# A four-layer graph network on one core: step 1's flag products moved to an iteration's end in TensorE's order

## The chip, the cores and the metric

The kernel runs on one core of a Trainium2 chip. The metric is the device time of one execution in microseconds (us); the kernel before has been run three times, and the median counts. A further execution was taken by the hardware profiler; all rows of views come from that one. TensorE does the matrix products, VectorE (DVE) and ScalarE (ACT) the work on rows, GpSimd (POOL) small powers and indirect DMAs, SyncE (SP) only issues DMAs.

## The reference

Four layers work on x (4096 rows of 256) with one adjacency matrix adj (4096 x 4096, zeros and ones), each as x = layernorm(x + layer(x)). Layer 1 is the one that matters here. Cut to it:

```python
for n in range(2):                       # STEPS
    q = Xa @ W1.T @ W2.T;  k = Xa @ W3.T
    probs = softmax(q @ k.T)             # 4096 x 4096
    A = probs where the largest of a row, added up, stay below 0.9, else 0
    A = A / sum(A)
    Xf = R @ Xf                          # R: adj with the unit matrix, rows scaled
    Xa = A @ Xa
    Z = Z + Xf @ U1[n].T + Xa @ U2[n].T
h = layernorm(X + Z)
```

The cut at 0.9 needs, for each row, the largest probabilities in order and their running sum.

## The kernel before

The rows are worked in 32 tiles of 128. Layer 0 comes first, then the two steps of layer 1 (n = 0 and n = 1), then layers 2 and 3. Only step 1 (n = 1) is touched.

**A tile's way in step 1.** `run_step` (L941) loops over i from -2 to 31, and three tiles are under way in each iteration. For tile i + 2 TensorE forms the logits (`logits_chunk`, L411), which ScalarE copies into a row block e (L412). For tile i + 1 VectorE looks for the largest values: `peak_groups` takes eight from each of 16 stretches (L430), `exp_rows` lets ScalarE form the exponentials (L453), `tops` takes the 64 largest in eight rounds (L525, L529), and `pick` adds them up and finds the threshold, how many equal values are too many, and whether the row can't be settled from 64 values. That last answer is `bad` (L561), one number for each of the 128 rows. `flag` and `settle` follow, see below. For tile i, whose e is settled by then, TensorE turns e by transposes (`turn`, L741; ScalarE copies the result, L744) and multiplies it with all rows of Xa (L766). `after` then mixes the result with U1 and U2 (L819, VectorE L821), two layer norms follow (L191 to L202, with GpSimd's power at L197), and the rows are written out. In the same iteration the product with adj (`neighbours`, L683, ScalarE's cast L680) for one tile is worked in.

**The order within an iteration.** `pieces` (L720) goes through eight groups, g = 0 to 7. In each it writes the logits of the group, the next group's transposes, the product of this group, and the group of adj; after that it calls what was entered for g by `at(g, ...)` in `run_step`. In step 1 the mix of the tile before is entered at 1, the next query (L391) at 1, `exp_rows` at 1, `tops` and `pick` at 2, `flag` at 4, `settle` at 5. A put-off job advances at 1 and 6.

**Flag and settle.** Rows with `bad` set are put off: they are gathered later, 128 at a time. `flag` (L579) must give each such row a place in a list. Two products of TensorE count them over the 128 rows: L589 with a matrix of ones (how many in the tile) and L590 with a triangle `before` (how many before this row). Both go into a half of one bank, `mm_bank`, whose halves are used in turn by queries, mixes and flags. VectorE forms the new total `sofar` (L592), `slot` (L596) and `slots` (L597), and GpSimd writes the row numbers into the list in memory by an indirect DMA (L603). `settle` (L638) does not need the counts: it removes surplus equal values from e (L655), and keeps what is over the threshold in four passes (L660). In step 1 the list is read at four points: after i = 7, 15, 23 and 30 `put_off` (L894) takes `base` from the total (L898), SyncE reads 128 entries (`take_rows`, L885), VectorE bounds them (L887), GpSimd gathers the rows (L809). Such a job then has its own query, logits, peak (L468), five probes (L495), tops, flag (L585) and settle, spread over the following iterations; its product comes at the next of the four points, for the last two after the loop. Beside those last two, TensorE has 32 products for layer 2 (`zu_tile`, L868).

**What sets the order on an engine.** The program is written in one order; the framework then plans a fixed order for each engine ahead of the run. It goes by an estimate of times: among the instructions that it takes to be ready, the one written earliest is placed next. So an instruction may stand earlier on its engine than it is written. `tc.keep_in_program_order(ins)` adds an edge without a semaphore: `ins` is placed behind the instruction of its engine that was written just before it.

Of the kernel before, what the change touches and what calls it, by code (L numbers as in the profile page):

```python
# [54 lines left out]
def gnn_stack(ctx, tc, x, adjt, adjn, w0, b0, w1, w2t, w3t, u1t, u2t, ln_g, ln_b, w2, b2, w3, b3, out):  # L55
# [3 lines left out]
    nc = tc.nc  # L59
# [3 lines left out]
    NLC = N // LC  # L63
# [20 lines left out]
    def half(bank):  # L84
        turns[bank] ^= 1
        return (mm_bank if bank == "mm" else acc_bank)[:, turns[bank], :]
# [90 lines left out]
    def transposed(*srcs):  # L177

        n = 2 * len(srcs)
        ps = ps_tr.tile([P, 4, P], F32, tag="tr", name="tr")  # L180
        for s, src in enumerate(srcs):
            for c in range(2):
                nc.tensor.transpose(ps[:, 2 * s + c, :], src[:, c * P : (c + 1) * P], ident)  # L183
        t = work.tile([P, 4, P], F32, tag="xt", name="xt")
        nc.scalar.copy(t[:, :n, :], ps[:, :n, :])  # L185
        return t
# [165 lines left out]
    with tc.tile_pool(name="l1", bufs=1, reuse_waits="tile") as l1:  # L352

        cur = {"late": False, "n": 0, "nef_done": False}
# [4 lines left out]
        ones_sq = l1.tile([P, P], F32, name="ones_sq")  # L359
# [25 lines left out]
        def query(xi, xt=None):  # L385

            if xt is None:
                xt = transposed(xi)
            ps = half("mm")
            for c in range(2):  # L390
                nc.tensor.matmul(ps[:, :P], wq_sb[:, c, :], xt[:, c, :], start=(c == 0), stop=(c == 1))  # L391
            up = upper(ps[:, :P])
            q = [work.tile([P, P], F32R, tag=f"q{k}", name=f"q{k}", bufs=3) for k in range(2)]
            nc.scalar.copy(q[0], up)
            nc.vector.tensor_sub(q[1], ps[:, :P], up)
            return q
# [17 lines left out]
        def logits_in(l):  # L414

            nc.vector.memset(l[:, N:], -1.0)
            return l

        def small(tag, w=1, dt=F32, bufs=2):
            if cur["late"]:  # L420
                return cur["lw"].tile([P, w], dt, tag=tag, name=f"{tag}_l", bufs=2 if w == 1 else 1)
            return work.tile([P, w], dt, tag=tag, name=tag, bufs=bufs)
# [34 lines left out]
        def peak_groups(st):  # L457

            st["cand"] = cand = small("cand", 8 * ngr, bufs=1)
            groups(st["e"], cand)  # L460
            st["m"] = m = small("m")
            nc.vector.tensor_reduce(m, cand, axis=AX.X, op=ALU.max)
            nc.vector.tensor_scalar(m, m, -1.0, None, op0=ALU.mult)
            st["base"] = None
# [114 lines left out]
        def flag(st):  # L579


            pb = half("mm")
            later = st.get("later")
            if later is None:
                nc.tensor.matmul(pb[:1, 0:1], st["bad"], ones_col, start=True, stop=True)  # L585
                st["nb"] = small("nbad", 1, I32)[:1, :]
                nc.scalar.copy(st["nb"], pb[:1, :1])
                return
            nc.tensor.matmul(pb[:, 0:1], ones_sq, st["bad"], start=True, stop=True)  # L589
            nc.tensor.matmul(pb[:, 1:2], before, st["bad"], start=True, stop=True)  # L590
            sofar, slot = small("sofar"), small("slot")
            nc.vector.tensor_add(sofar, later["base"], pb[:, 0:1])  # L592

            i = st["tile"]
            at, rows_i = slots_of[cur["n"]][:, i : i + 1], ids[:, i : i + 1]
            nc.vector.scalar_tensor_tensor(slot, pb[:, 1:2], later["base"], spare, op0=ALU.add, op1=ALU.subtract)  # L596
            nc.vector.scalar_tensor_tensor(at, slot, st["bad"], spare, op0=ALU.mult, op1=ALU.add)  # L597
            later["base"] = sofar
            if i == NT - 1 and cur["n"] == 0:

                st["to"] = to = small("to_last", 1, I32, 1)
                nc.vector.scalar_tensor_tensor(to, st["bad"], float(P), rows_i, op0=ALU.mult, op1=ALU.add)
            nc.gpsimd.indirect_dma_start(  # L603
                out=list_d[cur["n"]], out_offset=bass.IndirectOffsetOnAxis(ap=at, axis=0), in_=rows_i, in_offset=None)
# [316 lines left out]
        def left_over(n, e, later):  # L921

            count = work.tile([P, 1], I32, tag="count_l", name="count_l", bufs=1)
            nc.vector.tensor_scalar(count, later["base"], float(P - 1 - LATER[n] * P), 0.0, op0=ALU.add, op1=ALU.max)
            nc.vector.tensor_scalar(count, count, P.bit_length() - 1, None, op0=ALU.arith_shift_right)
            v = nc.values_load(count[0:1, 0:1], min_val=0, max_val=NT - LATER[n])
            with tc.For_i(0, v, 1) as k:
                cur["late"] = True
                st, xg = take_rows(n, bass.ds(k * P + LATER[n] * P, P), e)
                all_logits(st, query(xg))  # L930
                peak(st)
                exp_rows(st)
                st["t"], st["left"], st["base"] = small("t_thr"), small("left"), None
                for _ in settle(st, True):
                    pass
                pieces(n, st, None, {})
                for f in after(n, st):
                    f()
                cur["late"] = False

        def run_step(n, es):  # L941
# [37 lines left out]
            for i in range(-2, NT):  # L979
                st = tiles.pop(i, None)  # L980
                cd = tiles.get(i + 1)
                nxt = None
                if i + 2 < NT:

                    nxt = {"tile": i + 2, "q": cur["qs"].pop(0), "e": logits_in(es[i % 2]), "later": later, "G": {}}
                    tiles[i + 2] = nxt
                if i + 1 == NT and n == 0:
                    for fs in last:
                        for f in fs:
                            f()  # L990
                    last = []
                    left_over(n, es[NT % 2], later)
                ops = {}

                def at(g, f, *args):
                    ops.setdefault(g, []).append(lambda: f(*args))

                for g, fs in zip((1, 2), last):
                    for f in fs:
                        at(g, f)  # L1000
                if 0 < i + 2 < NT - 1:
                    turned = []
                    g = 1 if n else 6
                    at(g - 1, lambda i, turned: turned.append(transposed(cur["xa"][:, i + 3, :])), i, turned)
                    at(g, lambda turned: cur["qs"].append(query(None, turned[0])), turned)
                if cd is not None:
                    peak_groups(cd)
                    at(1, exp_rows, cd)
                for job in jobs:
                    at(1, advance, job)  # L1010
                if cd is not None:
                    rounds = 8 if n else KEPT // 8
                    at(2, tops, cd, rounds)
                    at(2, pick, cd, rounds)
                    at(4, flag, cd)
                    if n == 0:
                        for k in range(8):
                            at(4 + k // 2, gather, cd, k)
                    else:
                        at(5, lambda cd: [None for _ in settle(cd)], cd)  # L1020
                for job in jobs:
                    if n and i + 1 == NT:
                        at(4, advance, job)
                    at(6, advance, job)
                if i + 1 == NT and n == 0:
                    cur["next"] = load_halves(es[1 - NT % 2], xf_d, nc.sync)
                if i < 0:
                    now = FIRST[n][i + 2]
                else:
                    now = [i + 2] if FIRST[n][1][-1] < i + 2 < NT else []  # L1030
                pieces(n, st, nxt, ops, now)
                last = [[f] for f in after(n, st)] if st is not None else []
                if i in starts:
                    k = starts[i]
                    if len(jobs) > (i == NT - 2):
                        last = finish(jobs.pop(0), last)
                    e = es[NT % 2] if k + 1 == LATER[n] else es[2]
                    jobs.append({"stages": put_off(n, k, e, later)})
                    if i < NT - 2:
                        advance(jobs[-1])  # L1040
# [185 lines left out]
```

## Time and profile before

| what | value |
|---|---|
| median of three runs | 3284.64 us (3282.99 to 3286.56) |
| profiled execution | 3212.81 us |
| its span, first to last instruction | 3211.1 us |
| mean granted TensorE clock in it | 0.97 |
| step 1's flag products, first and last start | 1389.6 and 2503.2 us |
| instructions L589 and L590 in both steps | 128 each (two passes a tile, 64 tiles) |

A view's row names the line of the kernel, the engine and the operation, then the tiles as out<-in; "x" is a count. PE is TensorE's matmuls and PEld its weight loads, which overlap them. In a timeline row the first number is the start in us from the span's start and the second the time taken; neighbouring instructions of a kind are one row. In brackets stands how long the engine was idle before it and what ended that. In the rows by stretch, each engine's busy time is followed by its count of instructions; after the five engines come the granted clock, the share of the DMA engines and GB/s. A line of a helper (L149, L183 and others) serves many callers.

### The profile page before, as it was taken

Reading aid. Unit: us, or ns where it says so; the run is one execution under the profiler, and the core shown is the slowest. Engines: PE = TensorE matmul, PEld = TensorE weight load, DVE = VectorE, ACT = ScalarE, POOL = GpSimd, SP = SyncE. Lnnn points to the kernel's source line nnn. Section 1 sums busy time; section 2 is a strip of 40 time slices with the busy share of each in tenths; the row PEclk is TensorE's granted clock in tenths of the full one; section 3 lists DMA queues with packets and bytes.
Section 4 is the critical chain, followed back from the end, with each engine's and each line's share of the span. In section 5 each row is a group of like instructions: output and inputs, shape, how many; then the busy total and the mean of one; then the engine's idle time right before and its main releaser. Section 6 shows DMA issues by size and latency. Waiting matters only on the chain. (4 is left out here: it accounts for less than half of the span.)

```text
span 3211.1 us, 45754 instructions
## 1 busy us (share of the span) xinstructions
PE 2949.0 (92%) x14376; PEld 2329.4 (73%) x14376; DVE 2289.4 (71%) x7161; ACT 1745.9 (54%) x2906; POOL 786.8 (25%) x915
## 2 busy tenths in 40 slices
PE   8999889999999996799989899989999796999998
PEld 3788667777777774578877777877788554887886
DVE  4666778888888875269979896988799664444444
ACT  3555655666666654365545454545555334666664
POOL 1121256677666763000000001000100100000000
PEclk9999999999999998899999999999999898999999
DMA  9995467777778774310001110111011234333332
GB/s 175 164 173 117 83 114 141 144 143 143 141 142 150 152 140 118 118 50 25 24 24 27 34 39 24 32 32 37 29 35 27 71 119 139 109 108 101 106 110 81
DMA packets 247872, 300.14 MB, mean 93 GB/s; under 512 B 34688, under 2 KB 201536, under 8 KB 247616
## 3 DMA queue, kind: packets, MB, share of 16 engines
q0 software_dynamic: 46576, 104.94, 22.9%
q1 hardware_dynamic: 188800, 180.93, 18.4%
q10 hardware_dynamic: 12240, 11.23, 1.1%
q8 instruction: 116, 1.90, 0.2%
q14 instruction: 140, 1.15, 0.2%
HBM read 331.17 MB, written 66.45 MB: 124 GB/s over the span
## 5 line engine op out<-in xcount | busy, mean ns | idle before, releaser
L683 PE MATMUL acc_r<-xh,adjq 128*128 128x512 f32 x2048 | 608.5, 428 | 27.7 <-ACT adjq L680 18.6
L766 PE MATMUL acc_bank<-xa,at 128*128 128x256 f32 x2304 | 565.6, 386 | 27.9 <-ACT at L744 27.3
L669 POOL DMA_INDIRECT G<-x_d,cols x512 | 496.1, 969 | 262.6 <-PE acc_bank L758 154.1
L680 ACT CAST adjq<-adj 128x512 fp32r<-128x512 fp8e4 x512 | 316.5, 620 | 386.5 <-PE acc_r L683 308.2
L766 PEld LDWEIGHTS acc_bank<-xa,at 128*128 128x128 f32 x2304 | 422.3, 193 | 88.2 <-ACT at L744 38.7
L683 PEld LDWEIGHTS acc_r<-xh,adjq 128*128 128x128 f32 x2048 | 376.0, 191 | 123.1 <-ACT adjq L680 45.4
L197 POOL TENSOR_TENSOR rstd<-ve,mhalf 128x1 f32<-128x1 f32 x168 | 103.1, 614 | 1337.8 <-DVE ve L195 1270.5
L430 DVE MAX8 cand<-e 128x8 f32<-128x256 f32 x1024 | 382.9, 415 | 65.0 <-ACT e L412 63.7
L412 ACT COPY e<-lg 128x512 f32<-128x512 f32 x552 | 319.5, 585 | 195.8 <-PE lg L411 191.9
L411 PE MATMUL lg<-kS,q 128*128 128x512 f32 x1104 | 398.2, 446 | 4.6 <-ACT e L412 4.5
L1106 ACT CAST a<-a 128x1024 fp32r<-128x1024 fp8e4 x256 | 267.9, 1048 | 156.7 <-PE acc L173 121.3
L758 PE MATMUL acc_bank<-G,dg 128*128 128x256 f32 x1024 | 288.5, 399 | 61.8 <-DMA G<-x_d,cols 48.2
L527 DVE FIND_INDEX8 cols<-top,e 128x8 uint32<-128x4096 f32 x64 | 282.8, 4419 | 0.0
L758 PEld LDWEIGHTS acc_bank<-G,dg 128*128 128x128 f32 x1024 | 195.1, 196 | 117.8 <-DMA G<-x_d,cols 65.9
L173 PE MATMUL acc<-xh,a 128*128 128x512 f32 x1024 | 255.0, 402 | 20.2 <-DMA a<-adj_d 15.5
L173 PE MATMUL acc<-y0h,a 128*128 128x512 f32 x1024 | 253.6, 401 | 0.0
L173 PEld LDWEIGHTS acc<-xh,a 128*128 128x128 f32 x1024 | 190.6, 189 | 63.8 <-ACT xh L149 23.0
L173 PE MATMUL acc<-yh,a 128*128 128x512 f32 x1024 | 233.7, 390 | 0.0
L744 ACT COPY at<-at_ps 128x512 f32<-128x512 f32 x296 | 173.5, 588 | 98.7 <-PE at_ps L741 97.0
L173 PEld LDWEIGHTS acc<-yh,a 128*128 128x128 f32 x1024 | 192.2, 188 | 39.6
L173 PEld LDWEIGHTS acc<-y0h,a 128*128 128x128 f32 x1024 | 188.1, 188 | 42.0 <-issue 0.6
L185 ACT COPY xt<-tr 128x256 f32<-128x256 f32 (+1 forms) x268 | 111.9, 425 | 189.8 <-PE tr L183 172.8
(287 smaller groups left out, 4588.0 us busy)
## 6 DMA issues: line engine op xcount, KB each, us to landing
adj<-adj_d SPq DMA_DIRECT2D x256, 128.0 KB
a<-adj_d SPq DMA_DIRECT2D x256, 128.0 KB
a<-in_adjt POOLq DMA_DIRECT2D x64, 256.0 KB
adj_d<-a SPq DMA_DIRECT2D x64, 256.0 KB
adjn<-in_adjn POOLq DMA_DIRECT2D x64, 256.0 KB
x_d<-x SPq DMA_DIRECT2D x64, 128.0 KB
xf_d<-xf_new SPq DMA_DIRECT2D x64, 128.0 KB
G<-x_d,cols POOLq DMA_INDIRECT x512
```

The lines of the kernel that those rows point to most:

```text
L173: nc.tensor.matmul(acc, a[:, j, :], halves(jt), start=(jt == 0), stop=(jt == NT - 1))
L411: nc.tensor.matmul(pl[:, :LC], q[k], kS[:, s], start=(k == 0), stop=(k == 1))
L412: nc.scalar.copy(l[:, s], pl[:, :LC])
L430: nc.vector.max(dst[:, 8 * g : 8 * g + 8], src[:, g * GW : (g + 1) * GW])
L527: nc.vector.max_index(st["at"][:, 8 * r : 8 * r + 8], t8, st["e"][:, :N])
L669: nc.gpsimd.indirect_dma_start(out=g, out_offset=None, in_=x1_d, in_offset=bass.IndirectOffsetOnAxis(ap=st["at"][:, k : k + 1], axis=0))
L680: nc.scalar.copy(a, cur["a8"][:, g % 2 * GP : (g % 2 + 1) * GP, :])
L683: nc.tensor.matmul(acc_r, a[:, j, :], xf[:, jt, :], start=(jt == 0), stop=False)
L744: nc.scalar.copy(at[:, :G, :], ps[:, :G, :])
L758: nc.tensor.matmul(acc_a, dg[:, k % 4, :], st["G"][k], start=(k == 0), stop=(k == KEPT - 1))
L766: nc.tensor.matmul(acc_a, ats[g][:, j, :], cur["xa"][:, jt, :], start=(jt == 0), stop=(jt == NT - 1))
L1106: nc.scalar.copy(a, a8)
```

## The change

In step 1 `flag` is entered at group 7, the last of an iteration, instead of group 4; step 0 keeps 4. And in step 1 the first of its two products is kept behind the TensorE instruction written just before it. The second product is not kept so. No instruction is added or removed. With `flag` go its VectorE operations and its list entry, which are now written behind `settle`.

```diff
@@ flag
-            nc.tensor.matmul(pb[:, 0:1], ones_sq, st["bad"], start=True, stop=True)
+            total = nc.tensor.matmul(pb[:, 0:1], ones_sq, st["bad"], start=True, stop=True)
+            if cur["n"]:
+                tc.keep_in_program_order(total)
             nc.tensor.matmul(pb[:, 1:2], before, st["bad"], start=True, stop=True)
@@ run_step
-                    at(4, flag, cd)
+                    at(NLC - 1 if n else 4, flag, cd)
```

## The prediction

> **What bounds the kernel now.** I read the page first. TensorE is the busiest engine of the whole span, and the slices say that this holds almost everywhere:
>
> ```profile
> PE 2949.0 (92%) x14376; PEld 2329.4 (73%) x14376; DVE 2289.4 (71%) x7161; ACT 1745.9 (54%) x2906; POOL 786.8 (25%) x915
> ```
>
> The change can only touch step 1, which by its first and last flag product runs from 1389.6 to 2503.2 us. So I next asked who TensorE waited for between 1340 and 2530 us (columns: waiting line, releaser, us in total, times, longest):
>
> ```profile
> PE acc_bank L766 <- ACT at L744: 26.7, 15, 5.7
> PE mm_bank L589 <- DVE bad L561: 26.1, 17, 11.1
> ...
> PE at_ps L741 <- DVE e L660: 6.5, 1, 6.5
> ```
>
> The product that is to be moved (L589) is the second largest wait there: 26.1 us in 17 waits. One of them is 11.1 us; the other 16 sum to 15.0 us, some 0.95 us each. Then I listed each of the 32 products with its neighbours. The first ten tiles never wait (their `bad` is 11 us old or more). The waits stand in the iterations that also carry a put-off job. This is one of them on the timeline (start, us, engine, line; in brackets the idle time before it):
>
> ```profile
> 2359.22 0.14 DVE L561 SCALAR_TENSOR_TENSOR bad<-left,bad 128x1 f32<-128x1 f32 x1
> ...
> 2359.42 0.38 PE L589 MATMUL mm_bank<-bad,ones_sq 128*128 128x1 f32 x2 [1.00 <-DVE bad L561]
> ...
> 2359.89 1.54 PE L766 MATMUL acc_bank<-xa,at 128*128 128x256 f32 x6
> 2360.06 0.16 DVE L592 TENSOR_TENSOR sofar<-sofar,mm_bank 128x1 f32<-128x1 f32 x1 [0.23 <-PE mm_bank L590]
> ...
> 2361.32 4.43 DVE L655 MATCH_REPLACE8 e<-match,e 128x4120 f32<-128x4120 f32 x1
> ...
> 2366.01 1.27 DVE L660 SCALAR_TENSOR_TENSOR e<-e,t_thr 128x1024 f32<-128x1024 f32 x1
> ...
> 2369.12 0.60 PE L741 MATMUL at_ps<-ident,e 128*128 128x128 f32 x4
> ```
>
> TensorE stands 1.00 us for `bad`, and only 9.2 us after it the next iteration starts with the transposes of the same tile's e (2369.12), whose first quarter VectorE finished at 2367.28: 1.8 us in hand. In eleven such tiles (10, 14, 15, 18 to 23, 28, 29) that margin is 0.2 to 0.7 us. So **a second wait on VectorE stands close behind the first**. The busy times from one flag product to the next say how full the engines are (columns: stretch, us, then PE, PEld, DVE, ACT busy):
>
> ```profile
> 1488.47:1516.94 28.47, 26.99 (x143) 22.67 (x142) 25.57 (x89) 15.01 (x25) 2.23 (x3) 1.00 0.09 24
> 1780.22:1820.84 40.62, 34.61 (x169) 28.52 (x169) 33.15 (x108) 19.29 (x32) 2.23 (x3) 0.96 0.24 33
> ...
> 2359.42:2395.50 36.08, 34.94 (x177) 29.20 (x177) 35.26 (x118) 19.07 (x33) 2.23 (x3) 1.00 0.11 34
> 2395.50:2431.15 35.65, 34.56 (x178) 28.98 (x178) 34.47 (x115) 19.64 (x34) 2.24 (x3) 1.00 0.12 38
> ```
>
> The first row is an early tile: TensorE is the bound. The last two are tiles with a job: VectorE is busy 35.26 of 36.08 us, more than TensorE. The second is a third kind: both have gaps (6.0 and 7.5 us), each waiting for the other in turn. VectorE's own waits in step 1 name this, and a further one:
>
> ```profile
> DVE h L821 <- PE mm_bank L819: 33.6, 12, 6.6
> ...
> DVE from_l L887 <- DMA to_l<-list_d: 15.1, 3, 5.4
> ```
>
> **What the skill says.** The Trainium skill, "PSUM — Partial Sum Buffer", section "Engine vs sequencer instructions": matmuls start and complete in program order. The trace agrees: the L766 behind the flag products starts at 2359.89, at once behind them, though its operands were there. "Perfetto Trace Analysis", section "Identifying the Most-Contended Engine": the engine to relieve is the one with the highest occupancy, and it can change over time; the rows above show such a change. "DMA: Bandwidth & Descriptors", section "Anatomy of one DMA — SWDGE (gpsimd) path": some 2.0 us of fixed cost for such a DMA. Here the trace differs for the list entry: issued by GpSimd at 1935.66, SyncE's read of the list behind it went out at 1943.62, some 8 us, and that is the figure I use.
>
> **The change part by part.** (1) **Flag products moved and pinned.** Nothing is added or removed: four matmuls per tile (L589 and L590, 2 passes each) cost 0.47 us of TensorE (2359.42 to 2359.89) before and after. They go from behind group 4 to behind group 7 of 8, in the trace about 8 us later (1488.47 against the next tile's first transpose at 1496.37). By then `bad` is 8 us old, so their wait is gone: **15.0 us of TensorE idle time is the most that can be had**. The 11.1 us wait is not part of it: the last 16 matmuls of that iteration (L766 from 2487.86) already stand before that product, so it is at the iteration's end now; behind it the transposes wait another 6.5 us for e. Only settling is late there.
>
> (2) **VectorE's order.** sofar, slot, slots (0.16, 0.21, 0.20 us) are now written behind settle instead of before it. Their wait for TensorE (0.23 us) goes too, as TensorE has finished the products by the time settle's four passes end (tile 19: transposes at 2062.13, last pass at 2065.20). So e comes 0.6 us earlier (0.57 us of small operations plus 0.23 of wait, less what they overlap). TensorE comes to the transposes 1.0 us earlier, e 0.6: with 0.2 to 0.7 us in hand the new wait at L741 is 0 to 0.2 us at first.
>
> (3) **What is late next.** In the seven VectorE-bound iterations (from 1702.80, 2017.89, 2054.32, 2324.81, 2359.42, 2395.50, 2431.15) its work per tile stays, and only its 0.25 us wait can go: 7 x 0.25 = 1.8 us. TensorE runs ahead until the margin at L741 is used, and waits there. In the nine others with a flag wait both engines have gaps, and a TensorE that is earlier brings L819 earlier, for which VectorE waits (33.6 us in 12). Per tile that is worth nothing at the least and 1.0 us at the most; I take the 0.6 us by which e is earlier: 9 x 0.6 = 5.4 us. Sum: **7.2 us**.
>
> (4) **List and queues.** GpSimd's list entry (L603) is moved by the 8 us, with settle in front of it: past one or two small powers (L197, 0.6 us each), which it could delay by its 1.0 us; the value is 0.3 us a tile at VectorE, hidden where TensorE bounds, and I take 0 (bounds 0 and 3 us). At the put-off starts (i = 7, 15, 23, 30) the list's read on SyncE (L885), VectorE's L887 and GpSimd's gather hang on that entry. The first gather, at 1642.12, would go out at 1650; the job's query stands at 1661.47, so 11 us of cover against 8. At the last start the gather moves from 2514.55 to some 2524, its query (2526.03) by 1 to 3 us; behind it the job's e was ready at 2617.3, and TensorE came for it at 2628.08: 10 us cover. Without that cover it would be 3 us. (5) **Half banks.** The next query writes the half that sofar and slot read. It stands 13 us behind the boundary (2074.95 against 2062.13): hidden; up to 1 us a tile without.
>
> (6) **Planning.** The framework plans every engine's order anew from the first moved product. No row prices this; like iterations (34.3 to 36.4 us with equal work) differ by 1 us, over 20 of them some 4 us either way. I take 0.
>
> The profiled execution took 3212.81 us (span 3211.1 and 1.7 around it); less 7.2 it gives 3205.6. The median of the runs is 3284.64, 2.2% longer, which no view explains; with 7.2 x 1.022 = 7.3 us the forecast is **3277.3 us**.
>
> **Rivals.** *VectorE is the pace throughout*: the wait only moves to L741, worth 1.8 to 4 us: 3281 to 3283. For it: the margins of 0.2 to 0.7 us. Against: VectorE's 33.6 us of waiting for TensorE. *Slower, by the late list entry*: L885 and L887 are planned on an estimate of the list's DMA that is already 5 us short (waits of 5.4, 5.3, 4.4 us; TensorE then idles 5.7, 6.2 and 2.7 us behind ScalarE, which waits for VectorE). If the entry goes 8 us later and L887 keeps its place, each start costs up to 8 us more, half of which TensorE's queued work covers: 3 x 4 and 3 at the last start, 15 us, less 5 of gain: 3295 us. It decides once L887's waits reach some 10 us each. Against it: L887 is planned behind the entry, and should move with it. *It doesn't do it*: only L589 is pinned; L590 needs the same `bad`, and may be planned early in its stead. Then 3284.6. Against: L590 now follows L589 in all 32 tiles.
>
> **How the numbers follow.** Forecast 0.58 (own range 3270 to 3282), VectorE's pace 0.14, late list 0.24, no effect 0.04. A measurement can tell about 0.2%, 6.6 us. Of the forecast's 0.58, 0.42 lie beyond it and 0.16 within; so faster 0.42, same 0.16 + 0.14 + 0.04 = 0.34, slower 0.24. Low end: all 15.0 us and 3 of planning, 3267. High end: the late list with 2 of planning, 3297.
>
> **What would show it.** Right: L589's wait falls to the one near 2500 us, L592's vanish, L741's wait for L660 grows from 6.5 to between 8 and 15 us, and L821's 33.6 us shrinks. Wrong: L887's waits over 10 us, L590 waiting for `bad`, or iterations of 1400 to 1630 us (28.2 us each, not touched in my sum) that change length.

## The result and the profile after

| | before | after |
|---|---|---|
| median | 3285.6 us (8 runs, 3281.6 to 3297.8) | 3273.33 us (8 runs, 3262.3 to 3279.2) |
| ratio | | 0.9954, 95% interval 0.9936 to 0.9972 |
| profiled execution | 3212.81 us | 3274.57 us |

The kernel is faster: by 12 us in the medians, by 0.46% in the ratio of the runs, whose interval leaves out 1. Forecast were 7.3 us. The two profiled executions say the opposite at first sight, 3212.81 against 3274.57 us. That comes from ahead of the change: step 1's first transposes start at 1348.8 us in the one and at 1415.3 in the other, although step 0 is planned alike in both (TensorE has the same order there). So only step 1 is compared below, from those transposes to the first product of layer 2: 1334.7 us in this profile of before, 1340.1 in a second one, 1329.4 after.

In the kernel after, lines from L590 on stand two further down (L592 is the second flag product, L594 `sofar`, L662 settle's passes, L743 the transposes, L889 the list's bounds). TensorE's waits from 1406 to 2596 us, the same part of the kernel as before (waiting line, releaser, us, times, longest):

```profile
PE acc_bank L768 <- ACT at L746: 26.7, 14, 6.2
PE mm_bank L589 <- DVE bad L561: 16.6, 6, 11.1
...
PE at_ps L743 <- DVE e L662: 13.6, 9, 6.5
PE tr L183 <- DMA xf_new<-xa_d,from_l: 6.4, 1, 6.4
```

The flag product waits 5.5 us in five tiles, beside the 11.1 at the end, where it waited 15.0 in 16. The transposes' wait for e has grown from 6.5 us in one to 13.6 in nine. And a row is new: TensorE waits 6.4 us, once, for rows that GpSimd gathers for a put-off job. VectorE's waits of the same time:

```profile
DVE h L823 <- PE mm_bank L821: 37.1, 9, 9.5
DVE from_l L889 <- DMA to_l<-list_d: 19.5, 4, 7.3
...
DVE sofar L594 <- PE mm_bank L592: 2.3, 8, 0.8
```

The list's wait grew from 15.1 to 19.5 us, the longest from 5.4 to 7.3; that for the flag products is down to 2.3. The tile whose end the prediction showed at 2359.42, in the timeline of after:

```profile
2426.68 1.28 DVE L662 SCALAR_TENSOR_TENSOR e<-e,t_thr 128x1024 f32<-128x1024 f32 x1
...
2428.52 0.39 PE L687 MATMUL acc_r<-xh,ident_r 128*128 128x512 f32 x1
...
2428.75 0.28 PE L589 MATMUL mm_bank<-bad,ones_sq 128*128 128x1 f32 x2
...
2428.89 0.36 PE L592 MATMUL mm_bank<-bad,before 128*128 128x1 f32 x2
...
2429.11 0.64 PE L743 MATMUL at_ps<-ident,e 128*128 128x128 f32 x4
...
2431.49 0.17 DVE L594 TENSOR_TENSOR sofar<-sofar,mm_bank 128x1 f32<-128x1 f32 x1
...
2432.71 1.02 POOL L605 DMA_INDIRECT list_d<-ids,slots  x1 [14.15 <-DVE slots L599]
```

The products stand last in the iteration, right ahead of the next transposes. Neither they nor `sofar` wait. The list entry now goes out behind settle's four passes.

### The profile page after: what moved, and what is told of

Same layout as the page of the kernel before. It is cut to its first block, busy times and chain, and to the rows that moved or that the text cites. A ratio compares the mean times of both kernels' runs of the same rounds, so it can differ in the third digit from the quotient of the medians.

```text
span 3272.8 us, 45751 instructions
## 1 busy us (share of the span) xinstructions
PE 2970.0 (91%) x14376; PEld 2333.9 (71%) x14376; DVE 2290.0 (70%) x7161; ACT 1744.8 (53%) x2906; POOL 782.6 (24%) x915
## 5 line engine op out<-in xcount | busy, mean ns | idle before, releaser
L685 PE MATMUL acc_r<-xh,adjq 128*128 128x512 f32 x2048 | 620.0, 432 | 32.1 <-ACT adjq L682 18.8
L430 DVE MAX8 cand<-e 128x8 f32<-128x256 f32 x1024 | 383.9, 417 | 85.1 <-ACT e L412 49.5
L173 PE MATMUL acc<-xh,a 128*128 128x512 f32 x1024 | 256.1, 403 | 20.5 <-DMA a<-adj_d 16.4
L411 PEld LDWEIGHTS lg<-kS,q 128*128 128x128 f32 x1104 | 184.5, 193 | 34.0 <-ACT e L412 11.2
```

The source lines that it names most:

```text
L173: nc.tensor.matmul(acc, a[:, j, :], halves(jt), start=(jt == 0), stop=(jt == NT - 1))
L411: nc.tensor.matmul(pl[:, :LC], q[k], kS[:, s], start=(k == 0), stop=(k == 1))
L430: nc.vector.max(dst[:, 8 * g : 8 * g + 8], src[:, g * GW : (g + 1) * GW])
L685: nc.tensor.matmul(acc_r, a[:, j, :], xf[:, jt, :], start=(jt == 0), stop=False)
```

## The experiments

All kernels below keep the line numbers of before, as the pin is written on L589's own line. Ratios are to the kernel before on the same chip, with 95% intervals; its medians were 3247.7, 3283.4, 3284.5 and 3248.3 us on the four occasions. "Step 1" is the stretch named above, from the run's profile. The "starts" are the put-off starts, i = 7, 15, 23 and 30, after which the list is read. In e4 to e10 the first product is pinned in all of step 1, also where flag stays at group 4. There the pin changes next to nothing: in e5, TensorE's order from tile 8 to 24 is the one of before, instruction for instruction.

| run | edit against before | ratio | step 1, us |
|---|---|---|---|
| e1 | none | 1.0004 (0.9991 to 1.0018) | 1340.1 |
| e2 | the change | 0.9960 (0.9946 to 0.9974) | 1326.9 |
| e3 | flag right behind settle, no pin | 1.0025 (1.0012 to 1.0039) | 1350.2 |
| e4 | change, starts stay at 4 | 0.9944 (0.9923 to 0.9965) | 1318.3 |
| e5 | change for i from 24 only, no start | 0.9986 (0.9974 to 0.9999) | 1334.9 |
| e6 | change for 8 to 23 only, no start | 0.9931 (0.9910 to 0.9953) | 1316.8 |
| e7 | change, starts at 3 | 0.9922 (0.9900 to 0.9943) | 1316.4 |
| e8 | flag at 3 everywhere, pinned | 0.9954 (0.9935 to 0.9974) | 1325.7 |
| e9 | flag at 4, starts at 3, pinned | 0.9976 (0.9962 to 0.9991) | 1328.9 |
| e10 | change for 17 to 22 only | 0.9969 (0.9956 to 0.9982) | 1328.4 |
| e11 | before, adj fetched in halves | 0.9936 (0.9913 to 0.9959) | 1329.8 |
| e12 | change, adj fetched in halves | 0.9914 (0.9891 to 0.9936) | 1317.8 |

**e1 and e2: before and after once more, on one chip.** No edit, and the change with the pin written as one line:

```diff
-            nc.tensor.matmul(pb[:, 0:1], ones_sq, st["bad"], start=True, stop=True)
+            total = nc.tensor.matmul(pb[:, 0:1], ones_sq, st["bad"], start=True, stop=True); cur["n"] and tc.keep_in_program_order(total)
...
-                    at(4, flag, cd)
+                    at(NLC - 1 if n else 4, flag, cd)
```

> The kernel before, unchanged, for a second profile of it. It asks whether the profile of before, 3211 us long where its timed runs took 3283 to 3298, is typical in step 1. The stretch from the first transpose of the keys (L1087) to the first product of layer 2 was 1334.7 us in before and 1329.4 us in after, 5.3 us less, where the medians differ by 12.3 us. Theory A (the gain lies in step 1 alone, 5 to 8 us, and the rest of the 12.3 is scatter of step 0, whose order on every engine is the same in both kernels): the second profile shows 1333 to 1337 us again for this stretch, and a step 0 that is some 66 us longer than in the first profile. Theory B (the first profile was short in step 1 too): 1340 us or more. Time against before: 1.000.

> The changed kernel again, written so that the line numbers stay those of before. Theory A: the stretch from the keys to layer 2 takes 1328 to 1331 us, 4 to 7 us less than in the kernel before beside it, and the median is 5 to 8 us lower (ratio 0.9975 to 0.9985). Theory B: the ratio is 0.9955 again and the stretch 10 to 15 us shorter than in the kernel before beside it.

Theory B held in both: 1340.1 us, and 13.2 us less with the change. The gain is real and nearly twice the forecast. I then cut step 1 where `bad` of a tile is ready. Tiles 0 to 8 take 243.2 (e1) and 244.3 us (e2): nearly unchanged. The largest piece is tiles 18 to 24. Here is their row of before (e1, the first block) and of the change (e2, the second) (stretch, us, then busy PE, PEld, DVE, ACT, POOL with counts; granted clock, DMA share, GB/s), and above it the one from tile 16 to 17, below it tiles 26 to 31:

```profile
1961.49:1990.11 28.62, 21.75 (x105) 18.32 (x106) 20.62 (x76) 10.15 (x15) 4.02 (x4) 0.88 0.05 14
2050.49:2270.54 220.05, 206.04 (x1014) 168.44 (x1014) 200.46 (x677) 116.45 (x196) 15.03 (x18) 0.98 0.15 35
2358.00:2535.78 177.78, 161.22 (x823) 134.69 (x823) 173.05 (x575) 87.58 (x148) 12.89 (x15) 0.98 0.12 30
```

```profile
1963.22:1993.11 29.89, 23.78 (x124) 20.32 (x124) 22.54 (x85) 11.22 (x17) 6.04 (x7) 0.94 0.12 22
2050.39:2262.69 212.30, 203.23 (x1026) 168.58 (x1025) 201.46 (x678) 116.23 (x197) 13.41 (x18) 0.99 0.17 35
2352.54:2529.78 177.24, 159.57 (x821) 134.55 (x820) 172.65 (x574) 87.61 (x148) 12.09 (x15) 0.98 0.14 30
```

Tiles 26 to 31 are VectorE-bound (173 of 178 us) and give 0.5 us, as little as forecast. Tile 16 to 17, behind a put-off start, costs 1.3 us more. Tiles 18 to 24 give 7.7. This is no scatter of one execution: before in its two profiles has 219.4 and 220.0 us there, after and e2 212.4 and 212.3. (The stretch from tile 10 to 16 does scatter: 229.3 us in after and 225.6 in e2, which are one and the same change. So no weight is put on it. Tiles 8 to 10 and tile 17 to 18 are some 3 us shorter each with the change and tiles 24 to 26 are 2.3 us longer, in both profiles of either kernel; no run takes these apart.)

The 7.7 us are not to be taken to the tenth. In e5, e8 and e9 TensorE has the order of before in tiles 18 to 24 too, and takes 216.8, 220.2 and 217.4 us there. The row of e5:

```profile
2082.70:2299.51 216.81, 203.65 (x1014) 166.77 (x1014) 200.44 (x677) 116.37 (x196) 15.00 (x18) 0.99 0.15 36
```

So the old order scatters by 3.4 us between executions, and the new one is 4.4 to 7.9 us shorter. What TensorE waited for in tiles 18 to 24, in e1 and in e2:

```profile
PE acc_bank L766 <- ACT at L744: 7.8, 3, 3.8
PE mm_bank L589 <- DVE bad L561: 5.1, 5, 1.2
```

```profile
PE acc_bank L766 <- ACT at L744: 3.3, 1, 3.3
PE at_ps L741 <- DVE e L660: 2.9, 4, 1.0
PE mm_bank L589 <- DVE bad L561: 1.6, 2, 1.1
PE mm_bank L585 <- DVE bad_l L561: 1.3, 1, 1.3
```

This is the surprise. The flag wait gives 3.5 us, and 2.9 of it is paid again at L741 and 1.3 at a job's own flag: **nothing is left of it**. What is gained between these two profiles is 4.5 us of another wait, L766 for ScalarE's copy at L744, and 2.8 us of busy time with nearly the same work (206.0 to 203.2). The wait holds in all: it is 6.4 to 7.8 us in the five profiles with the old order and 3.3 and 3.4 with the change. The busy time doesn't: it is 203.7 us in e5 with the old order. The timeline of before shows where such a wait comes from:

```profile
2163.80 6.76 PE L683 MATMUL acc_r<-xh,adjq 128*128 128x512 f32 x27
2170.39 1.04 PE L741 MATMUL at_ps<-ident,e 128*128 128x128 f32 x8
2171.18 0.48 PE L683 MATMUL acc_r<-xh,adjq 128*128 128x512 f32 x1
2175.46 0.80 PE L766 MATMUL acc_bank<-xa,at 128*128 128x256 f32 x1 [3.79 <-ACT at L744]
```

```profile
2168.92 0.62 ACT L680 CAST adjq<-adj 128x512 fp32r<-128x512 fp8e4 x1 [0.43 <-PE acc_r L683]
2174.30 0.62 ACT L680 CAST adjq<-adj 128x512 fp32r<-128x512 fp8e4 x1 [4.76 <-DMA adj<-adj_d]
2174.83 0.58 ACT L744 COPY at<-at_ps 128x512 f32<-128x512 f32 x1
```

The first block is TensorE, the second ScalarE. At the iteration's boundary the plan of before puts 27 adj products in a row (35 from the last product with Xa to the transposes). They use up the tiles of adj that had been fetched, ScalarE's next cast waits 4.76 us for the next one, and the copy that TensorE needs stands behind that cast. With the flag moved, the plan comes out differently: its four longest such runs in these tiles, ahead of a transpose or a product with Xa, are 14, 18, 27 and 43 products, where they were 22, 24, 35 and 59. The 2.8 us of busy time are the clock: it stands at half speed for 10.2 us in these tiles before (3.4 and 6.8, beginning at 2133.0 and 2173.9, each within or right behind one of the two longer L744 waits) and for 3.4 us with the change. In e5 and e9, with the old order, it is 3.4 and 6.8 us, so the clock's part is not shown to come from the change. The Trainium skill has this in "TensorE: Matmul & The Clock Gate", section "What's actually happening": the clock goes to half after an idle window of some 3.4 us and back after a busy one. The traces agree with the length: pieces of half speed in step 1 are multiples of 3.41 us, from 3.41 to 20.48. But here a wait of 2.8 us, less than the window stated, was followed by half speed too (2133.0).

**e3: the late place without the pin.** The flag is written behind settle in group 5, and its products may be placed early.

```diff
-                    at(4, flag, cd)
+                    n or at(4, flag, cd)
...
-                        at(5, lambda cd: [None for _ in settle(cd)], cd)
+                        at(5, lambda cd: [None for _ in settle(cd)], cd); at(5, flag, cd)
```

> Step 1's flag at group 5, written right behind settle, not pinned: VectorE's order of the change (settle first, then sofar, slot, slots), with TensorE's products only one group later than before. Theory of the wait (the gain comes from TensorE no longer standing for bad): TensorE's place is nearly that of before, so L589 still waits 10 us or more in short waits, and at most a third of the gain is there: 0 to 3 us. Theory of VectorE's order (the gain comes from e being ready 0.6 us earlier in the tiles that are bound by it): half of the gain or more, 4 us and up, with L592 no longer waiting. Theory of the plan (any new order of step 1 moves the time by some us): anything from 8 us faster to 8 us slower, without relation to either wait.

It is 8 us slower: outside what the theories of the wait and of VectorE's order gave, and at the edge of planning's range. L589 still waits 23.1 us in step 1 and L592 10.5; L887 waits 19.6 for the list, as with the change. L821's wait rose from 34.9 to 43.3 us. The late place without the pin gains nothing; how much of the loss is the list isn't taken apart.

**e4 and e7: the put-off starts keep their early list entry.**

```diff
-                    at(4, flag, cd)
+                    at(NLC - 1 if n and i not in starts else 4, flag, cd)            # e4
+                    at((3 if i in starts else NLC - 1) if n else 4, flag, cd)        # e7
```

> The change, but in the four iterations after which the list is read (i = 7, 15, 23, 30) flag stays at group 4, as before. In the profile of after, VectorE's waits for the list (L887 there) grew from 15.1 to 19.4 us, and TensorE got a new wait of 6.4 us for the gathered rows at the first of these points. Theory of the late list entry (my rival, as a part of the truth: it takes back some of the gain): the wait for gathered rows is gone, L887's waits fall to 15 us or less, and the kernel is 4 to 8 us faster than the change. Against it: VectorE's wait is planned behind the entry and moves with it, so that nothing is to be had: within 2 us of the change.

> As the run with the list's points at group 4, but flag stands at group 3 in those four iterations. Theory of the late list entry: the list's read at i = 7 and 23 still waited 5.9 and 5.1 us there, and an entry one group (3 to 4 us) earlier takes that much off each wait and 2 to 5 us off the time (ratio 0.9930 to 0.9940). Rival (VectorE's wait is planned behind the entry and moves with it; what the four iterations gave came from TensorE's place): L887's waits stay at 5 to 6 us, same time within 2 us.

e4: an early list entry at the starts gains. Step 1 is 8.6 us shorter than in e2, L887's wait falls from 19.4 to 11.0 us, and tile 16 to 17 takes 23.7 us for 29.9. The ratios (0.9944 and 0.9960) say the same with less weight, as their intervals overlap. But the gain is more than the change had lost there: in e1 tile 16 to 17 takes 28.6 us. At that start the entry goes out 6.0 us behind its `bad` in e1, 11.6 in e2 and only 1.6 in e4, so e4 doesn't just put back the place of before. TensorE's wait for the gathered rows is gone as well, but with little effect: a wait of 6.2 us for L744's copy stands there instead (6.4 in e1), and tiles 8 to 10 take 80.1 us for 81.4. Tiles 24 to 26, behind the third start, stay at 90.4 us for 89.9, so what they lost is not the list. e7 added nothing that can be told: L887's waits are 5.7, 4.5 and 0.5 us, 10.7 for 11.0. What is left there doesn't hang on the entry. Its ratio is the lowest of the moves of flag, but from another chip than e4's, and the intervals overlap.

**e5, e6 and e10: the change for some tiles alone.** The condition in front of `else 4` is, in this order:

```diff
+                    at(NLC - 1 if n and i >= 24 and i not in starts else 4, flag, cd)
+                    at(NLC - 1 if n and 8 <= i < 24 and i not in starts else 4, flag, cd)
+                    at(NLC - 1 if n and 17 <= i <= 22 else 4, flag, cd)
```

> Flag at group 7 only in the last tiles (i from 24 on, but not at i = 30); before that at group 4 as in the kernel before. In these tiles VectorE is busy 97% of the time; with the change their flag waits went from 4.4 us to none, and the stretch from tile 26 to tile 31 still took 177.2 us against 177.8. Forecast's theory (where VectorE is the bound, taking TensorE's wait away gives only VectorE's own wait of 0.25 us a tile): 0 to 2 us faster than before, ratio 0.9994 to 1.0000. Rival (each flag wait that goes is a microsecond won, wherever it stands): 4 us or more, ratio 0.9988 or less.

> Flag at group 7 only for i from 8 to 23, not at i = 15 and 23; elsewhere at group 4. These tiles hold 11 of the 16 short flag waits and those iterations in which TensorE and VectorE wait for each other. Forecast's theory (the gain comes from the tiles in which both engines have gaps): all of what flag at group 7 with the list's points at group 4 gave (ratio 0.9944), within 2 us: 0.9940 to 0.9955. Rival (the gain is spread over all tiles, or comes from the early tiles' order): half of it or less, ratio 0.9972 or more.

> Group 7 (pinned) only for i = 17 to 22, six iterations in which TensorE and VectorE wait for each other in turn; all others stay at 4. If the wait that is removed is what gains, those tiles give back the 7 to 8 us that they gave in the change's own profile (tiles 18 to 24: 220.0 us to 212.3), with the half-speed time there falling from 10 us to 3 or 0: ratio 0.9970 to 0.9980. By the prediction's own term (0.6 us each) it is 3.6 us, ratio 0.9985 to 0.9992. The four starts stay as they are before: L887's waits 15 to 17 us.

e6 has all of the gain: 0.9931, below the range given, though its interval reaches into it. e10 has the forecast gain with six iterations alone: 0.9969, tiles 18 to 24 take 212.1 us, and the half-speed time there is 3.4 us. Its L887 waits 16.4 us, as before. That shows where the gain lies, but not that it is the flag wait's: in these tiles of e10 the flag wait is 3.5 us less than in e1, 3.0 us are paid at L741, and the 7.8 us of waiting for L744 are gone, with 2.7 for late casts (L683) in their place. e5 is unclear by its time: 0.9986, with an interval that reaches nearly to 1. In its profile the VectorE-bound tiles 26 to 31 take 178.2 us, no less than the 177.8 of before, so they are not where a gain could come from.

**e8 and e9: earlier instead of later.**

```diff
-                    at(4, flag, cd)
+                    at(3 if n else 4, flag, cd)                          # e8
+                    at((3 if i in starts else 4) if n else 4, flag, cd)  # e9
```

> The opposite of the change: in step 1 flag at group 3, one group earlier than before, pinned. Theory of TensorE's wait: TensorE comes to L589 one group (3.5 us) earlier in all 16 tiles with a wait, so the short waits grow from 15 us to 40 us or more, and what VectorE can't give back is lost in the tiles with gaps on both sides: 4 to 15 us slower, ratio 1.001 to 1.005. Rival (VectorE sets the time of bad, TensorE's work behind it fits in later, so that the wait's size is of no matter): within 3 us of before, though the waits grow.

> Only the iterations of the put-off starts (i = 7, 15, 23, 30) get flag a group earlier (3 for 4); all others stay at 4. If the earlier list entry at the starts is what made group 3 everywhere faster by 0.46%, this does the same: ratio 0.9945 to 0.9970, L887's waits fall from 16.5 us to about 11, and the stretch from tile 16 to 17 from 28.6 us to below 25. If that gain came from the other tiles, or from planning as a whole, the ratio is 0.9980 to 1.0010 here, though L887's waits fall alike.

e8 refuted both of its theories: 0.46% faster with L589's waits still at 27.9 us, not over 40. In the tiles that wait, the plan places the product where `bad` is ready, at 3 as at 4; so the flag wait stayed, and the gain has another source. e9 looked for it in the starts. Its row from tile 16 to 17:

```profile
1994.33:2015.74 21.41, 20.89 (x111) 17.87 (x112) 20.49 (x75) 10.59 (x15) 3.24 (x4) 1.00 0.07 19
```

28.62 us in e1 are 21.41 here, as in e8 (21.40): TensorE's idle time fell from 6.9 to 0.5 us and the clock from 0.88 to 1.00 of full. L887 waits 10.9 us. The ratio of 0.9976 lies between the two forecasts, and its interval meets both; the profile's mark is met. An earlier entry at the starts goes with 7 us in one place: it goes out 1.6 us behind `bad` here at i = 15, for 6.0 in e1. It is not shown to be all of e8's gain: tiles 8 to 10 take 81.9 us in e8 and 84.2 in e9, for 84.5 in e1.

**e11 and e12: take away the late adj.** In step 1 a tile of adj holds one group instead of two, in six buffers for three, so the same memory is given back in smaller parts.

```diff
-            if g % 2 == 0:
-                cur["a8"] = cur["w"].tile([P, 2 * GP, P], F8, tag="adj8", name="adj8", bufs=3)
-                nc.sync.dma_start(cur["a8"], adj8_d[i][:, g * GP : (g + 2) * GP, :])
+            if g % (w := 2 - cur["n"]) == 0:
+                cur["a8"] = cur["w"].tile([P, w * GP, P], F8, tag="adj8", name="adj8", bufs=6 // w)
+                nc.sync.dma_start(cur["a8"], adj8_d[i][:, g * GP : (g + w) * GP, :])
...
-            nc.scalar.copy(a, cur["a8"][:, g % 2 * GP : (g % 2 + 1) * GP, :])
+            nc.scalar.copy(a, cur["a8"][:, g % w * GP : (g % w + 1) * GP, :])
```

> The kernel before, flag at 4 and no pin, but in step 1 the tiles of adj are fetched one group at a time into six half-size buffers instead of two groups into three, so that the same memory is given back and filled again earlier; VectorE's and GpSimd's orders stay as they are, TensorE's nearly. Theory C (much of the change's gain in tiles 18 to 24 is not the flag wait, which only moves to e, but two ScalarE casts that wait for adj while TensorE waits behind them, and the half-speed stretch after each): L680's waits for adj fall from 24.3 us to below 12, TensorE's for L744 from 29.0 to below 22, tiles 18 to 24 from 220 us to 211 to 215, with L589's waits still at 26, ratio 0.990 to 0.997. If the flag wait itself is what gained, tiles 18 to 24 stay at 218 to 220 us and the ratio is 0.999 to 1.002.

> The change together with the finer fetch of adj. Theory C: the change and the finer fetch take away partly the same waits, so that the change adds little on top: this kernel's ratio is lower than that of the finer fetch alone by 0.0005 to 0.002 and not by the 0.0045 of the change alone. If the flag wait is what gained, the two add up: lower by 0.004 to 0.005.

e11, with the flag where it always was, is 0.64% faster (some 20 us, of which the one profiled step 1 shows 10.3). TensorE's waits in its tiles 18 to 24:

```profile
PE mm_bank L589 <- DVE bad L561: 5.4, 5, 1.2
PE acc_bank L766 <- ACT at L744: 4.9, 2, 2.5
PE acc_r L683 <- ACT adjq L680: 0.5, 1, 0.5
```

The flag wait is whole, 5.4 us, and L744's is down from 7.8 to 4.9. These tiles take 216.3 us, 3.7 less than in e1 and just above the range that I had given. But e5 took 216.8 there with the same order of TensorE and the old fetch, so this can't be told from scatter. Where the finer fetch does gain is tiles 10 to 16: 220.1 us, against 224.7 to 228.9 in the four profiles with the same order and the old fetch (before, e1, e5, e10). L683's wait for the casts is 9.2 us there in e1 and 0.2 in e11. Two of my marks failed: over step 1 the casts' wait for adj fell to 17.5 us, not below 12, and L744's hardly at all (29.0 to 28.4); what fell there is L683's wait for the casts, 12.8 to 3.8.

e12 is lower than e11 by 0.0022, about half of the change alone and somewhat over my range. In its profile tiles 18 to 24 take 211.4 us, 4.9 less than in e11, tiles 10 to 16 take 221.1, and step 1 as a whole 12 us less than in e11. By the profiles the two changes gain in different tiles, the finer fetch in 10 to 16 and the moved flag in 18 to 24, which speaks for adding up; the times (intervals of 0.0023 either way) point to a half. So theory C is not shown. In the timeline of tiles 18 to 24 TensorE does stand behind a copy that stands behind a late adj, and these waits shrink with the change; but a kernel that fetches adj more finely didn't shorten these tiles by more than scatter. That the late adj is the cause there is a reading of the timeline, and no run takes it apart further.

## Why the prediction was right, and where not

- **Direction and size.** Faster was right; 12 us for 7.3 is within the range. That the sum came near is partly luck: 5.4 of its 7.2 us were put down to a cause that gave less, and gains and costs of the new plan that it took as 0 came on top.
- **Step 1, the most to be had.** 15.0 us of flag waits were there; 9.5 went. 5.5 us stay in five tiles (for example 1.52 us at 1802.50): there TensorE reaches the product with the rest of the adj work still behind it, 7 to 12 us ahead of the transposes. The pin says what is in front of the product, not what is behind it. L590 did follow L589; the rival that nothing would happen is out.
- **Step 2, failed in part.** L592's wait fell from 11.2 to 2.3 us (e1, e2). But e was not 0.6 us earlier. From the end of `bad` to the end of e's first quarter, tile 21 takes 7.13 us in e2 for 7.98 in e1, tiles 19 and 20 take 7.13 for 7.32, tile 18 takes 7.26 for 7.18. Where the small operations go, VectorE mostly has a search for the next tile (L430, 0.42 us) in their place. In tiles 18 to 23 together e comes 1.7 us earlier, not six times 0.6. The margins of "0.2 us" (0.15 in tiles 10, 14 and 18) were also read too large: the transposes of tile 31, which waited 6.5 us for e, start 0.15 us behind it too, so there was nothing in hand. The new waits at L741 were to be 0 to 0.2 us at first; six of the eight are 0.7 to 1.0 us (e2).
- **Step 3, the failed term.** "TensorE then waits at L741" was right: 6.5 to 13.6 us, within the 8 to 15 given. So were the VectorE-bound tiles: 0.25 us each were forecast, tiles 26 to 31 gave 0.5 in five. But the "9 x 0.6 = 5.4 us" of the coupled tiles had the wrong cause. There too the flag wait only moved (3.5 us gone, 4.2 back in tiles 18 to 24), as the rival "VectorE is the pace" had it. These six iterations gave 7.7 us all the same, as L766's waits for a copy behind a late cast went. The first two of them, which the prediction counted as VectorE-bound, gave nothing (70.7 us in e1, 70.9 in e2); the gain lies in the four behind them. Of the coupled iterations from tile 11 to 14 nothing can be told, as tiles 10 to 16 scatter by 4 us. L821's 34.9 us, which were to shrink, came out at 33.2.
- **Step 4, taken as 0.** It was not covered: L887 waited 3 us more, and the first start made TensorE wait 6.6 us for the gathered rows (e2). The gather did go out some 9 us later: 23.6 us behind its `bad` in the first profile of before, 32.5 after. But its first reader is not the query (L391) to which the 11 us of cover were counted; it is TensorE's L183 at 1654.84, 6.6 us ahead of that. And the new plan had TensorE at L183 7.4 us earlier, 28.9 us behind `bad` for 36.3. The time lost is small all the same: tiles 8 to 10 are shorter with the change (81.4 us for 84.5), as a wait of 6.4 us for L744 went there, and at the second start tile 16 to 17 is 1.3 us longer (e1, e2). The 8.6 us that e4 gains are not all the price of the late entry, since 6.2 of them lie at the second start, where e4's entry is earlier than before's. The slower rival had a wait that exists, but not its size: no wait of L887 reached the 10 us from which it was to decide, the longest was 7.4.
- **Step 5** left no trace of a cost. **Step 6, planning, taken as 0 within 4 us,** is where most of the gain that can be placed is: a change of four small matmuls moved the adj products of whole iterations. The iterations of 28.2 us, as forecast, did not change.
- **The factor of 1.022** on the gain was groundless: the first profile of before was 29 us shorter than the second (e1) ahead of step 1, and only some 5 in it.

## What to carry to other kernels

A wait that is taken from one engine is not a gain until the next wait of that engine has been looked at: here most of it came back 7 to 10 us later, in front of e. Where a framework plans the order, look at what else the plan moves, above all at what stands in one queue in front of a copy that the busiest engine needs; in this kernel smaller tiles of adj (0.9936) are worth about as much as the change (the intervals overlap), both together give 0.9914, and the change without the late starts 0.9922 to 0.9944. All three together were not tried. When an instruction is moved, its list entry or other DMA goes with it; leave those early whose reader is near. And before a gain in one stretch is put down to an edit, look whether another run has that stretch in the old order: here five such profiles gave the size of the scatter.

## What the runs showed of the hardware

- In step 1 the clock is at half speed in pieces of 3.41 us or a multiple of it, most of them at idle times of TensorE, some of which are as short as 2.3 us (e12, the wait that ends at 1807.4). A wait of a given length doesn't settle it: in one place of the same order a wait of 3.69 us had a piece of 6.83 us (e1, ending at 1943.5), and one of 3.67 us had none (before, ending at 1914.2). As half of a piece is lost at the most, the wait of 2.8 us in e1 cost up to 1.7 us more, that of 3.8 us up to 3.4.
- The same planned order differs from one execution to the next: by 4 us in the six iterations from tile 10 to 16 between after and e2, with 23.9 us of half speed against 13.7, and by 3.4 us in tiles 18 to 24 among the five profiles with the old order. A single profile can't show a gain of that size; one that returns in each of several can be believed.
- From chip to chip it differs more. Ahead of step 1 TensorE's order is the same in all 14 profiles. That stretch took 1363 to 1384 us in the four profiles of one chip (e1 to e4), 1402 to 1421 in the six of another (e5 to e10), and 1373 and 1373 on a third (e11, e12). For the first profiles of before (1348.8) and after (1415.3) the chip is not on record. So times are compared on one chip.
